# A residual product written back into its input tile, with one pool of 23 tiles in place of 6 and 4

## The chip, the core and the metric

The kernel runs on one core of a Trainium2 chip. A core has a matrix engine (PE, with its weight loads shown apart as PEld), a vector engine (DVE), a scalar engine (ACT), GpSimd (POOL) and a sync engine (SP); each takes its instructions in order. Sixteen DMA engines move data between the chip's main memory (HBM) and the core's on-chip memory (SBUF). Products land in PSUM, from where DVE takes them.

In this kernel SP and ACT compute nothing: they only issue DMAs, SP the loads of `x`, ACT everything else. The metric is the device time in microseconds, the median of several runs. The profile is of one execution; its span runs from the first to the last instruction.

## What is computed

For each of 128 samples, a 128 x 1024 float32 matrix `x[b]` gets added to it the product with one of eight 128 x 128 matrices, chosen by the sample's subject number:

```python
w = weights[subjects]                       # (128, 128, 128) out of (8, 128, 128)
out = jnp.einsum('bct,bcd->bdt', x, w)
return x + out                              # (128, 128, 1024) float32
```

So 64 MiB come in and 64 MiB go out, and the weights add 0.5 MiB.

## The kernel before

The channel `c` lies on the 128 partitions. Work goes in pairs of samples: the outer loop (L58) runs 64 times over `b0`, and each pass loads one tile `xt` of two samples, 1 MiB (L60, issued by SP), and stores one tile `ot` of two samples, 1 MiB (L83, issued by ACT). The eight subject matrices are loaded once into `w_all` (L47), after the subject numbers `given` (L45); both are issued by ACT. Three small DVE instructions (L52 to L56) bring the numbers into range.

Within a pair the inner loop takes the two samples one after the other. POOL reads the sample's number into a register and copies the chosen matrix into a tile `w` of its own (L72). PE multiplies it with the two halves of the sample's 1024 columns (L75; the trace has each of these matmuls as two, so four a sample and eight a pair), into a PSUM tile `ps` of 128 x 1024. DVE adds `ps` and the sample's half of `xt` and writes the sum into its half of `ot` (L82).

The pools say how far things may run ahead of one another: six tiles for `xt` (L39), six for `w` (L40), four for `ot` (L41), four for `ps` (L42). With six `xt` tiles, load 7 goes into the tile of load 1, and must wait until the last reader of load 1, the second addition of pair 1, is done. With four `ot` tiles, pair 5's additions wait until store 1 has landed.

No order is written out by hand. The tile framework follows the reads and writes of each tile, puts every engine's instructions in an order, and inserts the semaphores through which they wait for each other. Loads, stores and the two small DMAs raise a semaphore when they land.

Of the kernel before, what the change touches and what calls it, by code (L numbers as in the profile page):

```python
"""out[b] = x[b] + weights[subject[b]].T @ x[b], for 128 samples of [C=128, T=1024].

The eight subject matrices stay in SBUF as [c, subject, d]. For each sample GpSimd reads the
subject's number into a register and copies that matrix into a tile of its own (a float32
stationary operand cannot be addressed by a register), TensorE multiplies in float32 with c on the
partitions, and VectorE adds the residual to the product while it takes it out of PSUM.
"""

# [1 line left out]

# [4 lines left out]

F32 = mybir.dt.float32
ALU = mybir.AluOpType

# Samples in one load or store: 1 MiB.
G = 2  # L20
# Columns of a product that fit one PSUM bank.
N = 512


@with_exitstack
def kernel(
    ctx: ExitStack,
    tc: tile.TileContext,
    x: bass.AP,
    subjects: bass.AP,  # L30
    weights: bass.AP,
    out: bass.AP,
):
    nc = tc.nc
    B, C, T = x.shape
    S, _, D = weights.shape

    const = ctx.enter_context(tc.tile_pool(name="const", bufs=1))
    xpool = ctx.enter_context(tc.tile_pool(name="xpool", bufs=6))  # L39
    wpool = ctx.enter_context(tc.tile_pool(name="wpool", bufs=6))  # L40
    opool = ctx.enter_context(tc.tile_pool(name="opool", bufs=4))  # L41
    psum = ctx.enter_context(tc.tile_pool(name="psum", bufs=4, space=bass.MemoryType.PSUM))  # L42

    given = const.tile([1, B], mybir.dt.int32, name="given")
    nc.scalar.dma_start(given, subjects.rearrange("(o b) -> o b", o=1))  # L45
    w_all = const.tile([C, S, D], F32, name="w_all")
    nc.scalar.dma_start(w_all, weights.rearrange("s c d -> c s d"))  # L47

    # Indices as the reference's indexing takes them: negative ones count from the end, and
    # those outside go to the nearest end.  # L50
    near = const.tile([1, B], mybir.dt.int32, name="near")
    nc.vector.tensor_scalar(near, given, -S, S - 1, ALU.max, ALU.min)  # L52
    wrap = const.tile([1, B], mybir.dt.int32, name="wrap")
    nc.vector.tensor_scalar(wrap, near, 0, S, ALU.is_lt, ALU.mult)  # L54
    index = const.tile([1, B], mybir.dt.int32, name="index")
    nc.vector.tensor_tensor(index, near, wrap, ALU.add)  # L56

    for b0 in range(0, B, G):  # L58
        xt = xpool.tile([C, G, T], F32, name="xt")
        nc.sync.dma_start(xt, x[b0 : b0 + G].rearrange("g c t -> c g t"))  # L60
        ot = opool.tile([D, G, T], F32, name="ot")
        for g in range(G):
            b = b0 + g
            s = nc.values_load(  # L64
                index[0:1, b : b + 1],
                engines=[mybir.EngineType.Pool],
                min_val=0,
                max_val=S - 1,
                skip_runtime_bounds_check_because="the index is clamped on the chip above",
            )  # L70
            w = wpool.tile([C, 1, D], F32, name="w")
            nc.gpsimd.tensor_copy(w, w_all[:, bass.ds(s, 1), :])  # L72
            ps = psum.tile([D, T], F32, name="ps")
            for t in range(0, T, N):
                nc.tensor.matmul(  # L75
                    ps[:, t : t + N],
                    w[:, 0, :],
                    xt[:, g, t : t + N],
                    start=True,
                    stop=True,  # L80
                )
            nc.vector.tensor_tensor(ot[:, g, :], ps, xt[:, g, :], ALU.add)  # L82
        nc.scalar.dma_start(out[b0 : b0 + G].rearrange("g d t -> d g t"), ot)  # L83


# [1 line left out]
_INS = ["x", "itok_B_0_7", "L0_cond_weights"]  # L87
_OUTS = [((128, 128, 1024), "float32")]


# [20 lines left out]
```

## Time and profile before

| what | value |
|---|---|
| time, median of 3 runs | 336.91 us (336.81 to 336.92) |
| span of the profiled execution | 336.0 us |
| HBM read, written | 67.63 MB, 67.11 MB; 401 GB/s over the span |
| PE matmul busy | 235.5 us (70%), 512 instructions, mean 606 ns |
| DVE busy | 152.1 us (45%); the 128 additions 1,221 ns each |
| POOL busy | 37.8 us (11%); the 128 copies 294 ns each |
| one load of `xt`, issue to landing | median 17.6 us |
| one store, issue to landing | median 17.4 us |
| DVE idle before the additions, waiting for stores to land | 109.5 us, 43 times |
| PE idle, waiting for the additions | 71.0 us, 53 times |
| POOL idle, waiting for PE | 254.2 us, 122 times |
| granted PE clock, mean | 0.987 |

How to read it: an engine's busy share is an average over the whole span. A page also cuts the span in 40 equal slices and gives for each the busy tenths of every engine, the mean busy share of the 16 DMA engines and the GB/s that they moved. A wait is listed under the instruction that came last; a DMA queue (SPq is that of SP) has waits of its own, which the engine's idle time doesn't show. "Landing" is when the data of a DMA has arrived and its semaphore has been raised.

### The profile page before, as it was taken

The numbers are of one execution on the slowest core, as the hardware profiler recorded it, in microseconds if no ns is written. First come the engines' busy times: TensorE is split into PE (matmuls) and PEld (weight loads), VectorE is DVE, ScalarE is ACT, GpSimd is POOL, SyncE is SP. The second block draws the span as 40 slices with busy tenths as digits, with TensorE's granted clock in tenths as the row PEclk, the third lists the DMA queues.
The fourth block names the chain that finished last, engine by engine and source line by source line (L and its number), as shares of the span: only waits on it lengthen the run. The fifth ranks groups of instructions, "written<-read, shape, count | busy, mean of one in ns | idle before, by whom it ended". The sixth has DMA issues, their size and how long they took to land.

```text
span 336.0 us, 2208 instructions
## 1 busy us (share of the span) xinstructions
PE 235.5 (70%) x512; PEld 93.7 (28%) x512; DVE 152.1 (45%) x131; POOL 37.8 (11%) x132
## 2 busy tenths in 40 slices
PE   0089999678678668668668668668768768767750
PEld 0034443223223223223223223223323323322310
DVE  0027754544544544544543543553543543553480
POOL 0021111111111111111111111111111111111000
PEclk9999999999999999999999999999999999999995
DMA  7937999999999999999999999999999999999996
GB/s 279 389 143 268 421 419 421 421 421 417 421 419 421 420 420 420 419 420 421 421 421 421 420 419 420 421 418 421 421 421 419 421 420 419 420 421 420 421 420 266
DMA packets 35870, 134.88 MB, mean 401 GB/s; under 512 B 2065, under 2 KB 3090, under 8 KB 35858
## 3 DMA queue, kind: packets, MB, share of 16 engines
q1 hardware_dynamic: 17408, 67.11, 49.4%
q10 hardware_dynamic: 18450, 67.64, 49.2%
q8 instruction: 4, 0.07, 0.1%
q14 instruction: 8, 0.07, 0.0%
HBM read 67.63 MB, written 67.11 MB: 401 GB/s over the span
## 4 chain that ended last, share of the span: by engine, by line
DMA 75%; DVE 8%; issue 8%; PE 5%; DVEq 1%; POOLq 0%; POOL 0%
DMA out_dram<-ot 75%; DVE ot L82 8%; PE ps L75 5%; DMA given<-in_itok_B_dram 0%; DVEq L107 0%; POOLq L64 0%; DVEq L82 0%; DVE index L56 0%; DVE wrap L54 0%; DVE near L52 0%; POOLq L72 0%; POOL w L72 0%
## 5 line engine op out<-in xcount | busy, mean ns | idle before, releaser
L75 PE MATMUL ps<-xt,w 128*128 128x512 f32 x512 | 235.5, 606 | 89.5 <-DVE ot L82 71.0
L82 DVE TENSOR_TENSOR ot<-ps,xt 128x1024 f32<-128x1024 f32 x128 | 151.4, 1221 | 173.4 <-DMA out_dram<-ot 109.5
L75 PEld LDWEIGHTS ps<-xt,w 128*128 128x128 f32 x512 | 93.7, 192 | 230.5 <-issue 120.0
L72 POOL COPY w<-w_all 128x128 f32 x128 | 37.6, 294 | 272.6 <-PE ps L75 254.2
L52 DVE TENSOR_SCALAR near<-given 1x128 int32<-1x128 int32 x1 | 0.2, 215 | 2.0 <-DMA given<-in_itok_B_dram 2.0
L56 DVE CUSTOM_DVE_ANT_0 index<-near,wrap 1x256 uint16<-1x256 uint16 x1 | 0.3, 278 | 0.0
L54 DVE TENSOR_SCALAR wrap<-near 1x128 int32<-1x128 int32 x1 | 0.2, 216 | 0.0
L98 POOL MEMSET const-float32-0.0<- 128x1 f32 x1 | 0.1, 98 | 0.2 <-issue 0.2
L98 POOL MEMSET const-bfloat16-1.0<- 128x1 bf16 x1 | 0.1, 101 | 0.0
L98 POOL MEMSET const-uint8-127<- 128x1 uint8 x1 | 0.1, 101 | 0.0
L98 POOL MEMSET const-float32-1.0<- 128x1 f32 x1 | 0.1, 98 | 0.0
## 6 DMA issues: line engine op xcount, KB each, us to landing
xt<-in_x_dram SPq DMA_DIRECT2D x64, 1024.0 KB, 17.6
out_dram<-ot ACTq DMA_DIRECT2D x64, 1024.0 KB, 17.4
w_all<-in_L_cond_weights_dram ACTq DMA_DIRECT2D x1, 512.0 KB, 16.5
given<-in_itok_B_dram ACTq DMA_DIRECT2D x1, 0.5 KB
```

Of the source, the lines that this page charges most:

```text
L52: nc.vector.tensor_scalar(near, given, -S, S - 1, ALU.max, ALU.min)
L54: nc.vector.tensor_scalar(wrap, near, 0, S, ALU.is_lt, ALU.mult)
L56: nc.vector.tensor_tensor(index, near, wrap, ALU.add)
L72: nc.gpsimd.tensor_copy(w, w_all[:, bass.ds(s, 1), :])
L75: nc.tensor.matmul(ps[:, t : t + N], w[:, 0, :], xt[:, g, t : t + N], start=True, stop=True,)
L82: nc.vector.tensor_tensor(ot[:, g, :], ps, xt[:, g, :], ALU.add)
L98: nc = _bacc.Bacc("TRN2", target_bir_lowering=False, num_devices=1)
```

## The change

The tile `ot` and its pool go. DVE writes the sum into the half of `xt` that it has just read, and the store takes `xt`. The pool of `xt` grows from 6 to 23 tiles of 1 MiB, that of `w` from 6 to 8. The loops, the shapes, the engines of all instructions and the sizes of all DMAs stay. Comments that the change takes out are left out here.

```diff
+BUFS = 23
...
-    xpool = ctx.enter_context(tc.tile_pool(name="xpool", bufs=6))
-    wpool = ctx.enter_context(tc.tile_pool(name="wpool", bufs=6))
-    opool = ctx.enter_context(tc.tile_pool(name="opool", bufs=4))
+    xpool = ctx.enter_context(tc.tile_pool(name="xpool", bufs=BUFS))
+    wpool = ctx.enter_context(tc.tile_pool(name="wpool", bufs=8))
...
         nc.sync.dma_start(xt, x[b0 : b0 + G].rearrange("g c t -> c g t"))
-        ot = opool.tile([D, G, T], F32, name="ot")
...
-            nc.vector.tensor_tensor(ot[:, g, :], ps, xt[:, g, :], ALU.add)
-        nc.scalar.dma_start(out[b0 : b0 + G].rearrange("g d t -> d g t"), ot)
+            nc.vector.tensor_tensor(xt[:, g, :], ps, xt[:, g, :], ALU.add)
+        nc.scalar.dma_start(out[b0 : b0 + G].rearrange("g d t -> d g t"), xt)
```

A tile of `xt` is now free for a later load only when the store that reads it has landed.

## The prediction

> **What bounds the kernel now.** I read the page's rows over time first, because they tell whether one limit holds all the way:
>
> ```profile
> DMA  7937999999999999999999999999999999999996
> GB/s 279 389 143 268 421 419 421 421 421 417 421 419 421 420 420 420 419 420 421 421 421 421 420 419 420 421 418 421 421 421 419 421 420 419 420 421 420 421 420 266
> ```
>
> Each slice is 336.0/40 = 8.4 us. From the fifth slice on the 16 DMA engines are full and move 417 to 421 GB/s; PE is busy 70% and DVE 45% of the span, so neither sets the pace. The 134.75 MB of the two large queues (67.11 and 67.64) must move before and after the change. Only a stretch in which the engines move less than 421 can be won: the third and fourth slice (143 and 268), the start and the end. I cut the dip finer, with the view of windows (the window; then its length, busy time and instruction count of PE, weight load, DVE and POOL; granted clock, DMA share, GB/s):
>
> ```profile
> 16.00:18.00 2.00, 0.00 (x0) 0.00 (x0) 0.00 (x0) 0.10 (x1) 1.00 1.04 402
> 18.00:20.00 2.00, 1.75 (x2) 0.83 (x3) 0.00 (x0) 1.28 (x5) 1.00 0.88 350
> 20.00:22.00 2.00, 2.00 (x4) 0.86 (x3) 0.00 (x0) 0.38 (x2) 1.00 0.00 0
> 22.00:24.00 2.00, 2.00 (x4) 0.74 (x3) 1.22 (x1) 0.29 (x1) 1.00 0.00 0
> 24.00:26.00 2.00, 2.00 (x6) 0.95 (x5) 1.23 (x1) 0.29 (x1) 1.00 0.00 0
> 26.00:27.00 1.00, 1.00 (x3) 0.38 (x2) 0.64 (x1) 0.29 (x1) 1.00 0.37 29
> 27.00:28.00 1.00, 1.00 (x4) 0.50 (x3) 0.59 (x1) 0.00 (x0) 1.00 0.83 37
> 28.00:29.00 1.00, 1.00 (x4) 0.45 (x3) 0.92 (x1) 0.29 (x1) 1.00 0.61 233
> ```
>
> Six loads and the weights are in by about 20 us; then the engines move nothing until the first store and the seventh load, and are at full rate from about 28.4. From 16 to 29 us the windows hold 1.80 MB (2 x 402 + 2 x 350 + 29 + 37 + 233, in GB/s times us); 421 GB/s for 13 us is 5.47. The missing 3.67 MB are **8.7 us**, all that deeper buffering can win before the tail. The tail is full at 416 to 424 GB/s until 332 us; then the 16 engines finish one after another.
>
> Who kept the seventh load? The DMA queue's own waits (total us, times, longest), and the issues around it in the timeline:
>
> ```profile
> SPq L60 <- DVE ot L82: 124.6, 51, 8.0
> SPq L60 <- DMA xt<-in_x_dram: 107.9, 49, 2.9
> SPq L60 <- DMA w_all<-in_L_cond_weights_dram: 11.5, 1, 11.5
> ...
> 5.95 0.37 SPq L60 DMA_DIRECT2D xt<-in_x_dram  x1
> ...
> 25.90 0.37 SPq L60 DMA_DIRECT2D xt<-in_x_dram  x1
> 25.91 0.47 ACTq L83 DMA_DIRECT2D out_dram<-ot  x1
> ```
>
> The longest wait on DVE, 8.0 us, is the buffer: load 7 needs the tile of load 1, which the second addition frees at 25.88. But before that the queue stood 11.5 us for the weights, which a load of x doesn't read. The explanation is in the trace's issue records, which name the semaphore that each landing raises: there are only eight, handed round in turn over loads and stores, and a DMA waits until the one eight places earlier in that order has landed. The order begins: indices, load 1, weights, loads 2, 3, 4, store 1, load 5; then store 2, load 6, load 7, store 3, load 8, store 4, load 9, store 5; then load 10. So load 6 waits for load 1 (hence its issue at 5.95), load 7 for the weights, load 8 for load 3, and **load 9 for store 1**, load 10 for store 2.
>
> **The change part by part.**
>
> *Loads no longer wait for DVE.* With 23 tiles the 8.0 us wait goes. What is late next is the turn of the semaphores. I take the order of the first 15 DMAs to stay as it is, since six buffers hadn't yet bent it: load 7 stands after store 2 there, not directly behind the addition that frees its tile. By hand:
> - Loads 1 to 6 and the weights as before; weights seen by SP at 17.9 (6.3 + 11.5). Load 7 issues at 17.9 instead of 25.9, load 8 half a microsecond later, as the first issues were spaced.
> - From the issue at 25.90 to full rate at 28.4 passed 2.5 us. So load 7 moves from 20.4, load 8 behind it. Reads alone ran at 402 to 413 GB/s (the windows 16 to 18 and 4 to 8); at 409 two times 1.049 MB take 5.1 us: until 25.5. The queue runs dry about 0.5 us before 20.4.
> - Store 1 still issues at 25.91: PE starts at 18.25 because the weights land then, and nothing in the change speeds that. It moves from 28.4 to 30.9 (1.049 MB at 421 are 2.49 us), landing seen about 31.3. Empty before it: 2.9 us.
> - Store 2 issues at 29.34 as before (the products come 3.43 us a pair), so moves from 31.8: 0.9 us empty.
> - Load 9 issues on store 1's landing at 31.3 and moves from 33.8, just before store 2 ends at 34.3. From there a pair is produced every 3.43 us and asks for 4.98 us of DMA time, so the engines stay full.
>
> Empty in all 0.5 + 2.9 + 0.9 = 4.3 us, and 9 us of reads at 409 in place of 421 cost 0.25 more. Against 8.7 before, **4.15 us** are won by this count. The 2.5 us are the term I trust least. The Trainium skill (page "DMA: Bandwidth & Descriptors", section "Latency and other measured facts") gives about 0.6 us to the first byte of such a DMA. The windows agree with that as far as it goes: from 26 us the engines are busy, share 0.37 and 0.83, but at 29 and 37 GB/s. By the rule store 1 would be at rate at 26.5: about 2.4 us empty and some 6 us won. The row is of this very DMA after an empty queue, so it decides; and when the queue isn't empty the delay may be hidden or longer. I take 3.9 us won.
>
> *The addition writes into the load's tile.* 128 instructions of 1,225 ns, same shape, same PSUM and SBUF reads: zero, beside full DMA engines. Its 43 waits for an output tile (109.5 us) go; in the steady stage what is late next is the arrival of loads, paced by the same 421 GB/s: zero. Writing in place adds a reader's wait: the addition must follow the products that read the same half. It does already, through `ps`. Whether the second half's products are now held by the first half's addition is a rival below.
>
> *A tile is free only when its store has landed.* A store takes 17.4 us from issue to landing, a load 17.6 (rows of the issues), with some 5 us of work between: 40 us at 4.98 us a pair are 8 tiles, of 23. Zero; a 9-tile pool would feel it.
>
> *Depth in the steady stage.* Zero. Here the skill speaks against the change: the page "Perfetto Trace Analysis" (section "Identifying Performance Opportunities") takes a gap that repeats on the saturated engine as the sign that buffers are short. No gap repeats here, so by the rule alone nothing is won: 336.9. The row shows one gap, once, of 8.7 us; I follow the row there and the rule everywhere else.
>
> *`wpool` 6 to 8.* POOL's wait for PE (254.2 us) shortens; the 294 ns copies already run ahead of PE under full DMA: zero.
>
> *Tail.* Last addition to end is one queue of stores at 418 to 424; loads come earlier by what was won, so it moves as a whole: zero, give or take 0.5.
>
> **Sum.** The profiled span is 336.0, with 0.9 outside it against the median 336.9. 336.0 - 3.9 = 332.1 span, **333.0** timed; own range 331.5 to 334.5, from 5.4 won (short start delay, load 9 a little earlier) to 2.4 won (slower starts, order bent a place).
>
> **Rivals.**
>
> *Loads run free.* If the new order puts more loads ahead of the first stores, or the turn doesn't hold them, reads continue through the dip. Then 8.7 less about 0.5 (reads at 409, load 7's gap) are won: 328.7. For it: with 23 tiles the order is made anew. Against: the 11.5 us wait shows the turn at work where no buffer was short. One load more (load 9 ahead of store 1's turn) gives 330.5; I count that here, 328.0 to 331.5.
>
> *It does nothing.* The turn eats all: if load 7's new place in the order lies behind store 1, the dip stays: 336.9. Against: load 7 visibly waited for the weights first, then for DVE.
>
> *The halves are chained: slower.* Both halves now are read and written in one tile. If the program orders accesses by whole tile, PE may start a pair's second product only after the first half's addition. The period of a pair becomes: three steps of 0.43 us and a matmul of 0.59 (1.88), addition 1.23, two hand-overs of about 0.05, then four steps of 0.43 (1.72): 4.93 us. It decides as soon as PE can't run at 3.43 and catch up, for 4.93 is the DMA's 4.98 with no slack behind the late start. First pair done at 26.6 (23.28, when the first addition ends, plus 2.1 and 1.23), 63 x 4.93 = 310.6, last store 2.5 + 2.5 + 0.4: 342.6 span, 343.5 timed. No view of the old trace shows which it is, since there no tile is both read by PE and written by DVE; the bounds are 0 and +6.6 us. I take zero: the two halves are disjoint ranges.
>
> **Chances.** Forecast 0.55; free loads 0.25; nothing 0.06; chained halves, with anything else slower, 0.14. Hence faster 0.80, within 0.2% (0.7 us, what a measurement of this kernel can tell from no change) 0.06, slower 0.14. The range joins the first two cases, 328.0 to 334.5, which hold eight in ten; 343.5 is left out.
>
> **What would show it.** Load 7 issued near 18 and load 8 behind it, load 9 held until store 1 lands: right. The third slice rises from 143 to about 380 GB/s, the fourth stays near 230 and not 420. An empty stretch of about 3 us ahead of the first store. PE continuous from 18 us at 3.43 us a pair: no chaining; PE gaps of 1.3 us inside each pair from the start: chained, and slower. If no gap is left and the time is below 330, the turn didn't hold the loads. If the steady rows leave 417 to 421, the steady stage isn't what I took it for.

## The result, and the profile after

Timed side by side, four runs each: 333.64 us (332.95 to 334.42) against 336.86 (336.51 to 336.92), a ratio of 0.9906 (95% interval 0.9886 to 0.9926). So 3.2 us were won, where 3.9 were forecast; 333.64 lies 0.6 above the forecast 333.0, inside the range of the forecast alone (331.5 to 334.5) and the wider one (328.0 to 334.5).

| | before | after |
|---|---|---|
| span of the profiled execution | 336.0 us | 331.5 us |
| HBM rate over the span | 401 GB/s | 406 GB/s |
| additions, mean of one | 1,221 ns | 1,225 ns |
| load, issue to landing, median | 17.6 us | 19.9 us |
| store, issue to landing, median | 17.4 us | 19.8 us |

The page of the changed kernel, its two DMA rows by slice (8.3 us each):

```profile
DMA  7997999999999999999999999999999999999996
GB/s 283 392 401 270 376 421 421 422 418 421 421 419 421 422 420 420 420 421 420 420 422 421 420 421 421 419 422 418 422 421 422 420 421 419 421 420 421 420 421 261
```

The third slice rose from 143 to 401, the fourth stands at 270 (268 before), and the fifth fell from 421 to 376. From the sixth to the last but one nothing changed. The DMA queue's own waits of the changed kernel (total us, times, longest):

```profile
SPq L63 <- DMA xt<-in_x_dram: 161.3, 35, 12.4
SPq L63 <- DMA out_dram<-xt: 87.8, 17, 13.1
...
SPq L63 <- DMA w_all<-in_L_cond_weights_dram: 11.6, 1, 11.6
```

And SP's loads between 17 and 30 us in its timeline (start, length, operation, number):

```profile
17.66 0.88 SPq L63 DMA_DIRECT2D xt<-in_x_dram  x2
...
29.08 0.37 SPq L63 DMA_DIRECT2D xt<-in_x_dram  x1
```

The loads' waits on DVE are gone. The wait for the weights is still there (11.6 us; 11.5 before) and now ends in the issue of loads 7 and 8, at 17.7 and 18.1. Then SP stands until 29.1: load 9 waits for store 1, as the turn of the eight semaphores says; the view of the queue's waits, asked for 18 to 30 us alone, puts it at 10.5 us:

```profile
SPq L63 <- DMA out_dram<-xt: 10.5, 1, 10.5
```

The trace's issue records show the same order as before: loads 6 and 7 between stores 2 and 3, load 9 eight places after store 1.

The windows of the changed kernel through that stretch (length, then busy time and count of PE, weight load, DVE, POOL; granted clock, DMA share, GB/s):

```profile
18.00:20.00 2.00, 1.96 (x3) 0.93 (x4) 0.00 (x0) 1.17 (x4) 1.00 1.02 403
20.00:22.00 2.00, 2.00 (x4) 0.92 (x3) 0.14 (x1) 0.92 (x4) 1.00 1.03 416
22.00:24.00 2.00, 2.00 (x5) 0.76 (x4) 1.28 (x2) 0.35 (x2) 1.00 1.03 412
24.00:26.00 2.00, 2.00 (x6) 0.95 (x5) 1.51 (x2) 0.49 (x2) 1.00 0.38 152
26.00:27.00 1.00, 1.00 (x3) 0.38 (x2) 0.75 (x1) 0.00 (x0) 1.00 0.99 406
...
28.00:29.00 1.00, 1.00 (x4) 0.47 (x3) 0.51 (x2) 0.00 (x0) 1.00 0.56 221
29.00:30.00 1.00, 1.00 (x3) 0.38 (x2) 1.00 (x1) 0.29 (x1) 1.00 0.62 250
...
31.00:32.00 1.00, 1.00 (x4) 0.47 (x3) 0.90 (x1) 0.06 (x1) 1.00 1.02 262
32.00:33.00 1.00, 1.00 (x3) 0.38 (x2) 0.61 (x1) 0.29 (x1) 1.00 1.09 238
...
34.00:36.00 2.00, 2.00 (x6) 0.86 (x5) 1.40 (x2) 0.37 (x2) 1.00 0.94 305
```

Three holes remain, and they differ in kind. At 24 to 26 us the engines are idle (share 0.38): in the packet records the loads end at 24.9, and store 1, issued at 25.06, has its first packets at 25.97. At 28 to 30 they are idle between stores 1 and 2, again for the 0.9 us from the issue of store 2 to its first packets. From 31 to 36 they are *busy*, share 0.94 to 1.09, and still move only 238 to 305 GB/s. Against 421 GB/s all windows from 16 to 40 us lack 4.27 us in this kernel and 8.70 in the one before: 4.4 of the 4.5 us by which the profiled span is shorter.

### The profile page after: what moved, and what is told of

The parts are those of the page before. It is cut to its first block, busy times and chain, and to the rows that moved or that the text cites. A ratio compares the mean times of both kernels' runs of the same rounds, so it can differ in the third digit from the quotient of the medians.

```text
span 331.5 us, 2130 instructions
## 1 busy us (share of the span) xinstructions
PE 235.4 (71%) x512; PEld 94.5 (29%) x512; DVE 157.5 (48%) x131; POOL 37.8 (11%) x132
## 4 chain that ended last, share of the span: by engine, by line
PE 44%; DMA 32%; DVE 14%; issue 5%; SPq 0%; POOLq 0%; POOL 0%
PE ps L77 44%; DMA xt<-in_x_dram 30%; DVE xt L84 14%; DMA out_dram<-xt 2%; DMA given<-in_itok_B_dram 0%; SPq L63 0%; POOLq L66 0%; DVE index L59 0%; DVE wrap L57 0%; DVE near L55 0%; POOLq L74 0%; POOL w L74 0%
## 5 line engine op out<-in xcount | busy, mean ns | idle before, releaser
L84 DVE TENSOR_TENSOR xt<-ps,xt 128x1024 f32<-128x1024 f32 x128 | 156.7, 1225 | 158.3 <-PE ps L77 158.3
## 6 DMA issues: line engine op xcount, KB each, us to landing
xt<-in_x_dram SPq DMA_DIRECT2D x64, 1024.0 KB, 19.9
out_dram<-xt ACTq DMA_DIRECT2D x64, 1024.0 KB, 19.8
```

What stands on the lines that cost most here:

```text
L84: nc.vector.tensor_tensor(xt[:, g, :], ps, xt[:, g, :], ALU.add)
```

## The experiments

**Which part of the change is it? Depth alone.** Separate tiles for loads and sums, 16 and 7:

```diff
-xpool bufs=6   wpool bufs=6   opool bufs=4
+xpool bufs=16  wpool bufs=8   opool bufs=7
```

> Depth alone: loads and sums keep separate tiles, 16 for xt and 7 for ot, 23 in all; wpool 8. My theory (loads 7 and 8 no longer wait for an addition, load 9 still waits its semaphore turn behind store 1) gives the same start as the changed kernel: load 7 issued near 17.7 us, load 9 after store 1 has landed, 333.6 us (333.0 to 334.5). Rival (writing in place is what helps): no gain, 336.9 us.

333.70 us against 337.15, ratio 0.9896 (0.9872 to 0.9919); load 7 issued at 17.7, load 9 at 29.4, after store 1. With the same depth, writing in place adds nothing that these runs can tell (333.64 against 333.70). It only makes room.

**How much depth?** The changed kernel with fewer tiles.

```diff
-BUFS = 23
+BUFS = 10   # and 8, and 6, in three kernels
```

> The changed kernel with 10 tiles, the memory of before (6 and 4). What was won needs only loads 7 and 8 to be free of the addition, so 10 tiles give what 23 give: 333.6 us (333 to 334.5). Rival (the depth of 23 counts; my own remark on record that a tile lives 40 us, 8 tiles of 4.98 us, and a 9-tile pool would feel it): slower than that, towards 336 us.

> The changed kernel with 8 tiles: load 9 needs the tile of load 1, so store 1's landing, which is what its semaphore turn waits for anyhow. Theory: start unchanged, and in the steady stage the 40 us of a tile's life are mostly waiting in a full queue, so fewer tiles only shorten the queue: 333.6 us (333 to 335). Rival (8 tiles times 4.98 us are just the 40 us, no slack): below 417 GB/s in the steady slices, 337 us or more.

> Writing in place alone, the pool left at 6 tiles. Load 7 now needs store 1 landed (near 31 us) in place of the addition (25.9): the dip grows by the store's 5 us, at rate from 31 us on: some 341 us (338 to 344), with the steady slices still at 420 GB/s. Rival (in place costs nothing at the start because of the turn): 336.9 us. If six tiles are too few in the steady stage as well: far above 344 us.

| tiles | time | before | ratio (95% interval) |
|---|---|---|---|
| 10 | 333.49 us | 337.32 us | 0.9894 (0.9874 to 0.9914) |
| 8 | 333.41 us | 337.32 us | 0.9887 (0.9868 to 0.9907) |
| 6 | 339.02 us | 337.32 us | 1.0057 (1.0035 to 1.0080) |

Eight tiles, two fewer than the ten of the kernel before, do what 23 do: only two more loads can go ahead of store 1's landing, whatever the depth. The 40 us that a tile lives are in good part time in a full queue; with eight tiles that queue is shorter (a load lands 11.4 us after its issue, in the median, in place of 19.9). With six, writing in place is a loss. The queue's waits of that kernel, where load 7 needs the tile that store 1 reads:

```profile
SPq L63 <- DMA out_dram<-xt: 283.5, 58, 22.8
```

All 58 reloads wait for a store, load 7 for 22.8 us; it issued at 28.98, 3.1 us later than before. Store 1 moves alone meanwhile, at 401 GB/s from 26 to 28 us, where the kernel before moved next to nothing, so only 1.7 us are lost. The 341 us expected took 5 us for the store, which alone on the engines needed 4.1 (issued at 24.89).

**Does the turn of the semaphores hold load 9?** First try: the first 12 loads written ahead of the loop, so that they stand ahead of store 1.

```diff
+    for b0 in range(0, AHEAD * G, G):
+        load(b0)
     for b0 in range(0, B, G):
-        xt = xpool.tile(...); nc.sync.dma_start(xt, ...)
+        if b0 + AHEAD * G < B:
+            load(b0 + AHEAD * G)
+        xt = tiles.pop(b0)
```

> The changed kernel, with the first 12 loads written ahead of the loop and each later load 12 pairs ahead, so that twelve loads stand before store 1 in the order in which the eight landing semaphores go round. Theory of the turn: load 9 now waits for an early load, not for store 1, no empty stretch is left before or after store 1, and the time is 328.9 us (328.0 to 330.5). Rival (load 9 was held by something else, such as a limit on the DMAs in flight): 333.6 us with the same empty stretch.

332.92 us, ratio 0.9888 (0.9867 to 0.9909), with the same rows as the changed kernel. This run decided nothing: the issue records show the semaphores in the same turn as before, store 1 still between loads 4 and 5. Here the framework's order did not follow the order in the source. The run only says that the edit doesn't reach what was to be tested.

Second try: take the early stores out of the turn. In this run the four stores issued by GpSimd raise semaphores outside the eight, as its issue records show.

```diff
-        nc.scalar.dma_start(out[b0 : b0 + G]..., xt)
+        store = nc.gpsimd if b0 < POOL_STORES * G else nc.scalar   # POOL_STORES = 4
+        store.dma_start(out[b0 : b0 + G]..., xt)
```

> The changed kernel, but stores 1 to 4 are issued by GpSimd. DMAs of GpSimd raise landing semaphores of their own, so the turn of the other eight now runs indices, load 1, weights, loads 2 to 6, then load 7 behind the indices, load 8 behind load 1, load 9 behind the weights, load 10 behind load 3: no early load stands behind a store. Theory of the turn: reads run on through 25 to 36 us, no slice of the start falls to 270 GB/s, and the time is 329.5 us (328.5 to 331). Rival (a limit on what is in flight, not the turn, held load 9): the dip after 25 us stays, 333.5 us or more.

329.29 us against 337.32, ratio 0.9763 (0.9743 to 0.9784). Its windows:

```profile
24.00:26.00 2.00, 2.00 (x6) 0.81 (x6) 1.50 (x2) 0.75 (x2) 1.00 1.01 401
26.00:28.00 2.00, 2.00 (x6) 0.91 (x5) 1.51 (x2) 0.39 (x1) 1.00 1.04 416
28.00:30.00 2.00, 2.00 (x6) 0.94 (x5) 1.51 (x2) 1.02 (x2) 1.00 1.01 403
30.00:32.00 2.00, 2.00 (x6) 0.80 (x6) 1.51 (x2) 0.30 (x2) 1.00 1.03 424
```

No hole is left. Loads 9, 10 and 11 issued at 17.8, 18.2 and 18.7 us, right after the weights. The tiles and the products are the same, and the stores came no earlier: store 1 was issued at 25.55 and had its first packets at 29.6, in the changed kernel at 26.0. So the other queue for the stores didn't fill the hole, the reads did. The turn had held load 9, worth 4.4 us against the changed kernel's 333.64 (4.8 us by the two ratios). Here the depth is used: fourteen loads were issued before store 1 landed, so the tiles beyond eight have loads to take.

**Is the root earlier still?** The dip stands at the start because the products wait for the weights until 17.5 us. One line, on the kernel before and on the changed one:

```diff
-    nc.scalar.dma_start(w_all, weights.rearrange("s c d -> c s d"))
+    nc.sync.dma_start(w_all, weights.rearrange("s c d -> c s d"))
```

> The kernel before with one edit: the load of the weights is issued by SP ahead of the loads of x, so its small packets don't share the engines with them. If the late start of the products is the root of the dip (weights in at 17.5 us), the weights land near 5 us, store 1 issues near 16 us while loads still run, and the dip is gone without a single tile more: 328.5 us (327.5 to 330). Rival (six loads are too few in any case): the dip stays, 335 us or more.

> The changed kernel with the same edit of the weights' load. If both edits remove the same dip, they don't add: 328.5 us (327.5 to 330), as with the edit alone. Rival (depth also wins something in the steady stage or the tail): 326 us or less. A further 0.9 us lost outside the span, as the changed kernel showed (333.28 timed against a span of 331.5, where before it was 336.9 against 336.0), would leave it above the edit alone.

329.01 us on the kernel before (0.9760, 0.9743 to 0.9777) and 328.71 on the changed one (0.9750, 0.9733 to 0.9768), both against 337.15. The issue of the weights in the kernel before, and in the same kernel with this edit (size, us to landing):

```profile
w_all<-in_L_cond_weights_dram ACTq DMA_DIRECT2D x1, 512.0 KB, 16.5
w_all<-in_L_cond_weights_dram SPq DMA_DIRECT2D x1, 512.0 KB, 4.2
```

And the page with this edit, by slice:

```profile
GB/s 269 409 413 421 421 421 421 422 418 422 418 422 421 420 421 422 418 422 420 422 420 422 417 422 420 420 420 422 420 421 420 422 420 419 421 421 420 422 420 276
```

The weights take 4.2 us to land in place of 16.5 and store 1 issues at 14.2. No slice between the first and the last falls below 409 GB/s, with six and four tiles. The two edits don't add up (0.3 us apart, intervals overlapping): they remove the same hole. These two are the fastest versions found, though the run with four stores on GpSimd (0.9763) can't be told apart from them.

Why the weights were slow: they come in packets of 512 bytes, the loads in packets of 4,096. Through 8 to 16 us the packet records of the changed kernel have some 90 of the one and 84 of the other in each microsecond, nearly one for one. The Trainium skill (page "DMA: Bandwidth & Descriptors", section "Queues, rings and completion order") says of the queues that an engine takes them in turn, packet by packet. A packet is there a group of descriptors, which need not be one record of the profile, so the trace agrees in the nearly equal counts but doesn't show how long one turn is. So half a megabyte has to wait for four megabytes of loads. Ahead of the loads on SP's own queue it doesn't (4.2 us). It isn't ACT as the issuer: issued by SP beside loads from ACT, in the last but one experiment, the weights still took 13.8 us.

**Whose is the slow start of load 9?** The changed kernel with the two issuing engines exchanged: all loads of `x` from ACT, the rest from SP.

```diff
-    nc.scalar.dma_start(given, ...);  nc.scalar.dma_start(w_all, ...)
+    nc.sync.dma_start(given, ...);    nc.sync.dma_start(w_all, ...)
-        nc.sync.dma_start(xt, ...)    # and the store: nc.scalar
+        nc.scalar.dma_start(xt, ...)  # and the store: nc.sync
```

> The changed kernel with the two issuing engines exchanged: loads from ACT, stores, indices and weights from SP. In the changed kernel load 9, issued at 29.1 us, brought its first packets at 32.6 and ran slowly until 36, while store 1, issued at 25.1, was at full rate by 26.0. If the slow start belongs to a load onto an empty queue, it stays with load 9 and the time is 333.6 us. If it belongs to SP's queue, it moves to store 1, load 9 starts within 1 us, and the time changes by one or two us either way.

330.37 us against 336.76 (0.9815, 0.9788 to 0.9842): faster by 3.3 us than the changed kernel, which I hadn't expected. Three of its windows:

```profile
28.00:30.00 2.00, 2.00 (x6) 0.95 (x5) 1.23 (x1) 0.29 (x1) 1.00 1.06 383
30.00:32.00 2.00, 2.00 (x6) 0.81 (x5) 1.50 (x2) 0.47 (x2) 1.00 0.90 248
32.00:34.00 2.00, 2.00 (x6) 0.90 (x5) 1.51 (x2) 0.41 (x2) 1.00 0.94 281
```

The slow stretch stayed with load 9 (issued at 28.04; 248 and 281 GB/s at 30 to 34 us), so it isn't SP's queue alone. The gain is a second matter, seen in the waits of the engines, of the changed kernel and then of this one:

```profile
PE ps L77 <- POOL w L74: 18.0, 1, 18.0
PE ps L77 <- POOL w L74: 15.4, 1, 15.4
```

That is PE's wait for its first weights: it began work at 15.4 us, not 18.0, since the weights landed at 14.6, not 17.3, and store 1 issued at 22.7, before the reads ran out. Over 16 to 40 us the windows give 386 GB/s in place of 346, which makes 2.3 of the 3.3 us; the rest was not traced. In the packet records 343 of the weights' 1,024 packets moved in the one microsecond from 5 us, before the turns became nearly equal. Why SP's queue gets that head start was not tested.

**What would the chained halves have cost?** The second sample's first half-product reads columns that the first addition has just overwritten, so PE must wait for DVE in each pair; that product is then made of other data.

```diff
-                    xt[:, g, t : t + N],
+                    xt[:, 0 if t == 0 else g, t : t + N],
```

> Prices the rival of the chained halves: in the changed kernel the second sample's first half-product reads the first sample's columns 0 to 511, which the first addition has just overwritten, so PE really must wait for DVE inside each pair (the second sample's product is then made of other data). Expected from the record: a pair takes PE 4.93 us instead of 3.43 from the start, PE shows a gap of some 1.3 us in each pair, no catching up behind the late start, 343.5 us (341 to 346). If the DMA's 4.98 us a pair hide the chain after all: 334 to 336 us.

354.98 us against 336.76, ratio 1.0527 (1.0491 to 1.0563). From the waits of its engines:

```profile
PE ps L77 <- DVE xt L84: 90.2, 64, 1.4
```

DVE's timeline, the first additions of two pairs that follow each other:

```profile
103.05 1.22 DVE L84 TENSOR_TENSOR xt<-ps,xt 128x1024 f32<-128x1024 f32 x1 [2.14 <-PE ps L77]
...
108.13 1.23 DVE L84 TENSOR_TENSOR xt<-ps,xt 128x1024 f32<-128x1024 f32 x1 [2.14 <-PE ps L77]
```

And two windows near the end:

```profile
300.00:320.00 20.00, 14.36 (x32) 5.56 (x31) 9.80 (x8) 2.35 (x8) 1.00 0.77 315
320.00:340.00 20.00, 14.37 (x33) 5.67 (x32) 9.79 (x8) 0.88 (x3) 1.00 0.51 203
```

One wait of 1.41 us in each of the 64 pairs, a pair every 5.08 us (103.05 to 108.13): the chain of PE and DVE is the bound. The loads run so far ahead that they end first, and what is left are stores alone at the pace of the pairs: 203 GB/s, where full slices move 421. The rival was a real one, but larger than I worked out: the hand-over PE, DVE, PE is 1.41 us where I had 1.33, the eight matmuls of a pair 3.67 where I had 3.60, so the period is 5.08 where I had 4.93 (63 pairs: 9.5 us). And store 1 issued at 28.1, so the first pair was 1.5 us later than my 26.6. In the changed kernel PE is continuous from 18 us to beyond 60, so its halves are not chained.

## Why the prediction was right, step by step

**What bounds the kernel; where there is something to win.** Right. The slices from the sixth on are the same; what was won lies between 16 and 40 us.

**Loads 7 and 8 go at 17.9, load 9 waits for store 1.** Right: 17.7, 18.1 and 29.1, and the run with four stores outside the turn shows that it was the turn. Load 9 went 2.2 us earlier than the 31.3 of the forecast, because store 1 moved and landed earlier than forecast.

**The size of the holes.** The sum was right (4.55 us lacking expected, 4.27 found), but by luck: three terms were off, and they cancelled.

| hole | expected | measured, from the windows |
|---|---|---|
| ahead of load 7 | 0.5 us | none: 403 and 416 GB/s |
| ahead of store 1 | 2.9 us | 1.3 us (24 to 26 us) |
| between stores 1 and 2 | 0.9 us | 0.9 us (28 to 30 us) |
| behind, until loads and stores are both full | 0 | 1.8 us (30 to 38 us) |
| reads at less than 421 | 0.25 us | 0.24 us (16 to 24 us) |

The 2.5 us from issue to full rate were the term that I trusted least, taken from one row for loads and stores alike, and that row was load 7's alone. In the packet records of the kernel before, load 7, issued at 25.90, had its first packets at 26.93; these sixteen took 0.3 to 1.6 us each, and full rate came only at 28.5. Store 1, issued beside it, had its first packet only at 28.92. (The windows count a packet's whole time where it begins, so the share of 0.37 from 26 us doesn't say that the engines were busy from 26 us on, as the prediction reads it.) A store that starts alone isn't so slow: in the changed kernel store 1 issued at 25.06 and had its first packets at 25.97, 0.9 us later, and store 2 likewise. The 0.6 us to the first byte of the Trainium skill (page "DMA: Bandwidth & Descriptors", section "Latency and other measured facts"), which I had set aside, is nearer to this than my row. Load 9, by contrast, needed 3.5 us to its first packets (29.1 to 32.6) and ran slowly for three more; store 2 beside it was slowed too. That I hadn't foreseen. Store 1 also issued 0.85 us earlier than in the profile before.

**From the sum to the time.** This is the term behind the 0.6 us, as far as the runs show. I set the span of the profiled execution (336.0) beside the median of the runs (336.9) and took 0.9 us as lying outside the span. Every run since lists both, and the difference is 1.7 to 1.9 us in each, for the kernel before as well (336.77 with a span of 335.0); its spans go from 334.4 to 336.2. So the profiled execution of before, whose own timed run isn't on record, was longer than a median one by some 0.9, and 1.8 had to be added: 336.0 - 4.15 + 1.8 = 333.65. That this falls on 333.64 is luck: the 4.15 came from terms that cancelled, and the changed kernel's runs spread over 1.5 us. I had also rounded 4.15 down to 3.9, with no row to say so. The spread of 1.8 us of the kernel before was not explained, as there is one trace of it; so it stays open whether the 0.9 lay in the dip, where a median execution would then have less to win, or elsewhere.

**The edits at zero.** In place: right by the run with separate tiles. Depth in the steady stage and `wpool`: right, unchanged slices. The remark that a 9-tile pool would feel it was wrong; 8 tiles feel nothing.

**The rivals.** Free loads, at 328.7: it didn't happen, and its price was right, as 329.29 shows where it was made to happen. Chained halves: didn't happen, priced 11.5 us too low.

## What to carry to other kernels

Before adding buffers to close a hole, follow the waits of the queue that is late beyond the first one named: here a wait for a buffer stood in front of a wait for a semaphore that had nothing to do with the data, and the second one took back half of the gain. Then ask what the hole is made of: one line that brought the late weights in first won 8 us with the old buffers, where 13 more tiles won 3 (and eight in place would have won the same). And read a single profiled execution against its own timed run before a median is put beside it.

## What the runs showed of the hardware

Engines that are busy and slow: while load 9 starts onto an empty load queue beside store 2, packets of 4 KB take 196 to 299 ns in the mean of each microsecond from 31 to 36, store 2's first and then the loads', in place of 159, and 238 to 305 GB/s pass at a busy share of 0.94 to 1.09. The kernels with 10, 8 or 6 tiles, with separate tiles, with loads written ahead, and with the queues exchanged show the same. Where a load starts while no store's data moves, as load 7 in the kernel before and load 10 in the chained one, the first packets come 1.0 us after the issue and take up to 1.6 and 1.0 us, and full rate comes 2.5 and 2.1 us after the issue. The kernels in which loads never run dry (weights first, four stores on GpSimd) have no such stretch. What causes it stays open.
